# Gathering part of the third layer's first seven tiles from a second table, ahead of the last block's rows

## The chip, the cores and the metric

The kernel runs on one core of one Trainium2 chip. The metric is the device time of one execution in microseconds (us), smaller is better. Beside the plain timed executions there is one execution recorded by the hardware profiler; all durations below come from that one.

## What is computed

Four graph layers over N = 4096 nodes with F = 128 features, each followed by a residual sum and a layer norm. The adjacency matrix `adj` is symmetric in its pattern and nearly empty: some eight neighbours per node beside the diagonal.

```python
x = layernorm(x + signed_attention(x, adj))      # layer 0
x = layernorm(x + chebyshev(x, adj))             # layer 1: three products with adj, twice
# layer 2: attention with 4 heads; only entries of adj count
h = (x @ weight.T).reshape(n, heads, f_out)
C = alpha_src[None] + alpha_dst[:, None]
tau = adj_t * exp(maximum(0.2 * C, C))
z = einsum('mnh,nhf->mhf', adj_t * tau / tau.sum(1), h)
x = layernorm(x + z + bias)
# layer 3
x = layernorm(x + x @ W_self + (adj @ x / deg) @ W_neigh)
```

In the title "third layer" is layer 2 of this listing, the attention.

## The kernel before

Nodes are cut into 32 tiles of 128 (`NT`), and into 8 blocks of 512 (`NB`, four tiles each). Layers 0 and 1 are dense products on TensorE that read `adj` from HBM in chunks of 1 MB. While they run, the kernel makes lists of the non-zero entries: for every column the six neighbours with the highest row index (`NEAR`), and the rest of all columns of a tile packed into three lists of 128 slots (`QT`). `lists.source[:, t, 0:9]` holds the row indices of tile t: 0 to 2 are the packed slots, 3 to 8 the six neighbours. An unused slot points at row N, which holds zeros and a very low score. `check` (L1565) looks over bounds that the lists rely on and sets a flag; if it is set, a second, general version of the network runs after this one.

`sparse_layers` (L1722) is the last part, and the change lies in it. Its engines follow an order that is written out by hand: every engine executes its instructions in the order in which Python emits them.

First comes the rest of layer 1: for each block `ib` eight chunks of `adj` times `w`, four products a chunk (L2050), collected in PSUM. `block_end(ib, p)` (L1746) then turns the sum of a block into the rows that the attention reads: ELU, transposes (L154), layer norm, a product with `W2S` (L1781), rows scaled by the norm (L1786), and a store of 512 rows of 132 floats into the DRAM tensor `table` (L1789, a DMA on ScalarE's queue). `block_end` is a generator with eight steps, and `one(chains)` advances it by one step after each chunk of the next block, so that its small steps lie between the products. For the last block (`ib` = 7) no products are left to put between.

GpSimd (POOL) meanwhile fetches `value` entries of the lists by indirect DMA: `pulls`, three a chunk, each followed by a one-element operation, `pause` (L1518, L1563). One more pause a chunk reads a tile that VectorE has just written (`known`), which holds POOL to the pace of the chunks.

Then the attention: a loop over 32 tiles. `gathers(t)` (L1815) issues nine indirect DMAs on POOL for tile t, each of which brings 128 rows of `table` into `got[t]` (four buffers); every second one is followed by a pause, and two of the pauses read the reciprocal `rd` of two tiles earlier and the newest sum `acc3`. `edges(t)` (L1837) turns `got[t]` into weighted rows, nearly all on VectorE (L1846 to L1858); its first operation that needs the gathered rows is L1850. `sums` multiplies them on TensorE (L1863), `divide` and `turn` finish the tile (L1870 to L1872, L159, L160), and `layer3_rows` and `layer3_product` use the new x for layer 3 (L1931: one product per tile with all of `adj`; VectorE adds the results up, L1944). Groups of tiles for layer 3 have 1, 1, 2, 4, 4, 4, 4, then 2 tiles each, and 1 and 1 at the end. Before the loop, four chunks of 1 MB for the first two groups are requested on ScalarE's queue (`columns` with `nc.scalar`, L1919). In the loop, `gathers(t + 2)` comes after the work on tile t, and `check` runs ahead of tile 3's work.

Of the kernel before, what the change touches and what calls it, by code (L numbers as in the profile page):

```python
# [11 lines left out]
F32 = mybir.dt.float32  # L12
# [5 lines left out]
ALU = mybir.AluOpType  # L18
AX = mybir.AxisListType
PSUM = bass.MemoryType.PSUM  # L20

P = 128
IB = 512
TB = IB // P
# [11 lines left out]
QT = 3  # L36
# [3 lines left out]
PAIRED = [0, 1, 2]  # L40
LAST = [0, 1]
FAR = [4, 5, 6, 7]
NONE = -1e30


@with_exitstack
def adj_resnorm_d4(ctx: ExitStack, tc: tile.TileContext, x_in, xT_in, adj, adjT, pairs, diag_in, w0g, w0gT, a0, w1a, b1a,
# [7 lines left out]
    nc = tc.nc  # L55
    N, F = x_in.shape
# [1262 lines left out]
    class Lists:  # L1319
# [3 lines left out]
        def __init__(self, whole, first, layer, own_entries):  # L1323
            enter = lambda **kw: whole.enter_context(tc.tile_pool(reuse_waits="tile", **kw))
            self.keep = keep = enter(name="lists", bufs=1)
            self.psum = first.enter_context(tc.tile_pool(name="ps_u", bufs=2, space=PSUM, reuse_waits="tile"))
            dram = enter(name="dram", bufs=1, space=bass.MemoryType.DRAM)
            self.table = dram.tile([N + 1, F + H], F32, name="table")
            self.tables = [dram.tile([N + 1, F], F32, name=f"rows{n}") for n in range(3)]
            self.spread = dram.tile([NB, P, TB * SLOTS], BF16, name="spread")  # L1330
            self.top = state.tile([P, NT, NB, 8], F32, name="top", tag="dv")
            self.at = keep.tile([P, NT - TB, NB, 8], U16, name="at")
            self.diag = own_entries
            self.last = None
            nc.scalar.dma_start(self.diag, diag_in)
            self.source = keep.tile([P, NT, NEAR + QT], I32, name="source")
            self.value = keep.tile([P, NT, NEAR + QT], F32, name="value")
            self.where = keep.tile([P, NT, QT], I32, name="where")
            units = len(PAIRED) * TB
            self.back = keep.tile([P, units, NEAR + QT], F32, name="back")  # L1340
            self.into = keep.tile([P, units, QT], F32, name="into_column")
            self.column = keep.tile([P, TB], I32, name="column")
            self.tile_column = keep.tile([P, TB, QT], I32, name="tile_column")
            self.bad = keep.tile([P, 4, NB], F32, name="bad")
            self.iota = keep.tile([P, P], F32, name="iota")
            self.slot = keep.tile([P, SLOTS], F16, name="slot")
            self.place = keep.tile([P, TB, QT], F32, name="place")
            self.first = keep.tile([P, NB, 8], F32, name="first")
            self.own = keep.tile([P, 1], F32, name="own")
            self.below = keep.tile([P, P], BF16, name="below")  # L1350
            self.row = keep.tile([P, TB, QT], I32, name="row")
            flat = lambda t: t.rearrange("p s r -> p (s r)") if len(t.shape) > 2 else t
            with tc.tile_pool(name="lists_i", bufs=1) as pool:
                i = pool.tile([P, SLOTS], I32, name="i")
                for t, pattern, base, step in ((self.slot, [[1, SLOTS]], 0, 0), (self.place, [[0, TB], [P, QT]], 0, 1),
                                               (self.first, [[IB, NB], [0, 8]], 1, 0), (self.own, [[0, 1]], 0, 1)):
                    n = flat(t).shape[1]
                    nc.gpsimd.iota(i[:, 0:n], pattern=pattern, base=base, channel_multiplier=step)  # L1358
                    nc.vector.tensor_copy(flat(t), i[:, 0:n])
                nc.vector.tensor_copy(self.iota, self.slot[:, 0:P])  # L1360
                nc.vector.tensor_scalar(self.below, self.iota, self.own, None, op0=ALU.is_gt)
                none = pool.tile([1, F + H], F32, name="none")
                nc.vector.memset(none, 0.0)
                nc.vector.memset(none[:, F:F + H], NONE)
                nc.scalar.dma_start(self.table[N:N + 1, :], none)
                zero = pool.tile([1, F], F32, name="zero")
                nc.vector.memset(zero, 0.0)
                for rows in self.tables:
                    nc.scalar.dma_start(rows[N:N + 1, :], zero)
            nc.gpsimd.iota(self.column, pattern=[[P, TB]], base=0, channel_multiplier=1)  # L1370
            nc.gpsimd.iota(flat(self.tile_column), pattern=[[P, TB], [0, QT]], base=0, channel_multiplier=0)
            nc.gpsimd.iota(flat(self.row), pattern=[[IB, TB], [0, QT]], base=0, channel_multiplier=0)
            self.idle = keep.tile([P, 2], F32, name="idle")
            nc.gpsimd.memset(self.idle, 1.0)
            self.work = layer.enter_context(tc.tile_pool(name="lists_w", bufs=1, reuse_waits="tile"))
            self.both_at = self.work.tile([P, units, NEAR + QT], I32, name="both_at")
            self.both = self.work.tile([P, units, NEAR + QT, 2], F32, name="both_ways")
# [187 lines left out]
        def check(self, psum, name):  # L1565

            worst = small.tile([P, 4], F32, name="worst")
            for n, most in enumerate((0.0, 0.0, float(MOST), float(SLOTS))):
                nc.vector.tensor_reduce(worst[:, n:n + 1], self.bad[:, n, :], AX.X, ALU.max)
                nc.vector.tensor_scalar(worst[:, n:n + 1], worst[:, n:n + 1], most, None, op0=ALU.is_gt)  # L1570
            both = small.tile([P, 2], F32, name="both")
            nc.vector.tensor_reduce(both[:, 0:1], worst, AX.X, ALU.max)
            units = len(PAIRED) * TB
            free = self.into.rearrange("p u j -> p (u j)")
            left, own = free[:, 0:units], free[:, units:2 * units]
            nc.vector.tensor_scalar(self.back, self.back, 0.0, None, op0=ALU.is_gt)
            nc.vector.tensor_reduce(left, self.back, AX.X, ALU.add)
            for n, c in enumerate(PAIRED):
                nc.vector.tensor_scalar(own[:, n * TB:(n + 1) * TB], self.diag[:, c * TB:(c + 1) * TB], 0.0, None, op0=ALU.is_gt)
                nc.vector.tensor_tensor(own[:, n * TB:(n + 1) * TB], own[:, n * TB:(n + 1) * TB], degrees[0][:, c * TB:(c + 1) * TB], ALU.subtract)  # L1580
            nc.vector.tensor_tensor(left, left, own, ALU.add)
            nc.vector.tensor_reduce(both[:, 1:2], left, AX.X, ALU.add)
            pb = psum.tile([1, 2], F32, name=name)
            nc.tensor.matmul(pb, ones, both, start=True, stop=True)
            most = small.tile([1, 1], F32, name="most")
            nc.vector.tensor_scalar(most, pb[:, 1:2], 0.0, None, op0=ALU.not_equal)
            nc.vector.tensor_tensor(most, pb[:, 0:1], most, ALU.max)
            nc.vector.tensor_tensor(flag, most, flag0, ALU.add)
# [133 lines left out]
    def sparse_layers(enter, lists, w, h0T):  # L1722
# [19 lines left out]

        warm = small.tile([P, 1], F32, name="warm")
        fresh = None

        def block_end(ib, p):  # L1746

# [29 lines left out]
            for half in range(2):  # L1777
# [8 lines left out]
                nc.vector.tensor_tensor(rows[:, two, :], pn[:, :, 0:F + H], scale.to_broadcast([P, 2, F + H]), ALU.mult)  # L1786
                nc.vector.tensor_tensor(near[:, two, :], pn[:, :, F + H:F + 2 * H], scale.to_broadcast([P, 2, H]), ALU.mult)
                fresh = rows[:, two.start, 0:1]
            nc.scalar.dma_start(table[ib * IB:(ib + 1) * IB, :].rearrange("(k p) f -> p k f", p=P), rows[:, tb, :])  # L1789
            e = l2.tile([P, TB, H], F32, name="e")  # L1790
            d = l2.tile([P, TB, H], F32, name="d")
            nc.vector.tensor_tensor(e, near[:, tb, :], rows[:, tb, F:F + H], ALU.add)
# [22 lines left out]
        def gathers(t, behind={}):  # L1815
            if t >= NT:
                return
            got[t] = l2.tile([P, E, F + H], F32, name="got", bufs=4)
            for j in range(E):
                nc.gpsimd.indirect_dma_start(got[t][:, j, :], None, table,  # L1820
                                             bass.IndirectOffsetOnAxis(ap=lists.source[:, t, j:j + 1], axis=0))
                if j % 2:
                    lists.pause(behind.get(j))
# [159 lines left out]
        with tc.manual_schedule(engines={mybir.EngineType.PE, mybir.EngineType.DVE, mybir.EngineType.Activation,  # L1983
# [3 lines left out]
            def one(queue, n=1):  # L1987
                while queue and n:
                    r = next(queue[0], queue)
                    if r is not queue:  # L1990
                        n -= 1
                    else:
                        queue.popleft()
# [49 lines left out]
            for ib in range(NB):  # L2043
# [3 lines left out]
                for n, c in enumerate(order):  # L2047
                    a = chunk(ld, adjT, ib, c)
                    for k in range(TB):
                        nc.tensor.matmul(p, w[:, c * TB + k, :], a[:, k, :], start=n == 0 and k == 0,  # L2050
                                         stop=n == NB - 1 and k == TB - 1)
                        if k == 1:
                            one(others)
                    one(chains)
                    for f in plan.pop(hook, ()):
                        f()
                    if known is not None:
# [6 lines left out]
                next(end)  # L2064
                chains.append(end)
            assert not plan and not others
            while chains:
                one(chains)
            for t0, n in groups[:2]:
# [87 lines left out]
```

## Time and profile before

| what | us |
|---|---|
| median of three timed runs | 1839.98 (1831.49 to 1844.66) |
| the profiled execution, whole | 1653.07 |
| its span (first to last instruction) | 1651.2 |
| layers 0 and most of 1 | 0 to 1000 |
| rest of layer 1, with block ends | 1000 to 1216 |
| attention and layer 3, POOL gathering | 1216 to 1590 |
| last tile, rest of layer 3, output | 1590 to 1651 |

The timed runs take 187 us longer than the profiled execution of the same program; nothing in the trace says where. The page of the profile gives each engine's busy time, the chain of work that ended last (followed back from the last instruction, each step to what released it), and the costliest groups of instructions. Over the whole span TensorE is busy 90%, VectorE 69%, POOL 50%. Those shares are means over stages with different limits, so the stage of the change has to be read by itself, from the timeline of each engine, in which a bracket names the idle time before an instruction and what ended it.

### The profile page before, as it was taken

How to read it: one execution, taken by the hardware profiler on the slowest of the kernel's cores; microseconds unless marked ns; L12 is line 12 of the kernel's file. 1: busy time of each engine (PE TensorE's matmuls, PEld its weight loads, DVE VectorE, ACT ScalarE, POOL GpSimd, SP SyncE). 2: the span in 40 equal slices, each digit the busy share in tenths (PEclk: the TensorE clock that was granted, in tenths of full speed). 3: DMA queues.
4: the chain of work that ended last, by engine and by line, in shares of the span. 5: the costliest groups of instructions: out<-in, count | busy, mean ns of one | idle time of the engine just before them, and what ended most of it. 6: DMA issues, size and time to landing. Idle time of an engine off the chain costs nothing.

```text
span 1651.2 us, 16460 instructions
## 1 busy us (share of the span) xinstructions
PE 1478.5 (90%) x4744; PEld 714.2 (43%) x4744; DVE 1138.4 (69%) x3203; ACT 385.5 (23%) x693; POOL 833.1 (50%) x1322
## 2 busy tenths in 40 slices
PE   6899999999999999999999999889927689788886
PEld 3344444544444444454444454444413344444444
DVE  5987655789887897988699950455336756556766
ACT  5776540010000011121200000222223111122234
POOL 0000000000242188848486888888648888888841
PEclk9999999999999999999999999999967798889988
DMA  9867776588888885867587888778665677678673
GB/s 374 342 256 301 246 271 233 179 277 299 316 315 320 309 285 195 281 210 274 177 296 248 291 278 305 252 265 287 241 151 153 189 259 244 219 239 278 218 192 95
DMA packets 106972, 419.30 MB, mean 254 GB/s; under 512 B 21556, under 2 KB 44088, under 8 KB 67064
## 3 DMA queue, kind: packets, MB, share of 16 engines
q1 hardware_dynamic: 59984, 360.01, 61.1%
q0 software_dynamic: 22656, 36.17, 8.6%
q10 hardware_dynamic: 24232, 21.98, 4.5%
q8 instruction: 39, 0.64, 0.2%
q14 instruction: 61, 0.50, 0.1%
HBM read 404.39 MB, written 13.70 MB: 253 GB/s over the span
## 4 chain that ended last, share of the span: by engine, by line
PE 46%; DVE 25%; POOL 14%; issue 6%; DMA 6%; ACT 3%; ACTq 0%; DVEq 0%; POOLq 0%
PE pacc L730 15%; PE pacc L423 12%; POOL got L1820 6%; PE pp L2050 5%; DMA got<-table,source 4%; PE pp L1931 3%; POOL got L1518 3%; DVE at L1397 3%; DVE top L1396 2%; POOL idle L1563 2%; DVE here L1556 1%; POOL value L1518 1%; DVE same L1317 1%; DVE gw L1856 1%; DVE acc L1944 1%
## 5 line engine op out<-in xcount | busy, mean ns | idle before, releaser
L1820 POOL DMA_INDIRECT got<-table,source x288 | 275.8, 958 | 88.8 <-issue 62.0
L1931 PE MATMUL pp<-chunk,xT 128*128 128x512 f32 x496 | 244.0, 633 | 1.4 <-ACT xT L1902 0.7
L730 PE MATMUL pacc<-chunk,x 128*128 128x512 f32 x512 | 222.6, 593 | 0.0
L1518 POOL DMA_INDIRECT got<-rows,source x180 | 182.8, 1016 | 67.6 <-issue 38.6
L423 PE MATMUL pacc<-chunk,hw 128*128 128x512 f32 x408 | 188.7, 607 | 0.8 <-DVE hw L466 0.7
L1358 POOL IOTA i<- 128x384 int32 (+3 forms) x4 | 1.0, 238 | 345.7 <-PE pden L411 329.8
L2050 PE MATMUL pp<-chunk,w 128*128 128x512 f32 x384 | 173.1, 600 | 0.0
L730 PE MATMUL pacc<-chunk,t 128*128 128x512 f32 x384 | 171.5, 597 | 0.0
L730 PEld LDWEIGHTS pacc<-chunk,x 128*128 128x128 f32 x512 | 96.0, 190 | 114.7 <-issue 114.6
L730 PE MATMUL pacc<-chunk,v 128*128 128x512 f32 x320 | 144.5, 597 | 0.0
L1396 DVE MAX8 top<-chunk 128x8 f32<-128x512 f32 x196 | 128.5, 677 | 14.1 <-DMA chunk<-in_adjT 14.1
L1931 PEld LDWEIGHTS pp<-chunk,xT 128*128 128x128 f32 x496 | 94.2, 203 | 91.2 <-issue 84.1
L1397 DVE FIND_INDEX8 at<-top,chunk 128x8 uint16<-128x512 f32 x196 | 133.1, 684 | 0.0
L1518 POOL DMA_INDIRECT both_ways<-in_pairs,both_at x108 | 106.6, 987 | 17.4 <-issue 17.1
L423 PEld LDWEIGHTS pacc<-chunk,hw 128*128 128x128 f32 x408 | 75.0, 192 | 92.1 <-issue 86.3
L1563 POOL TENSOR_TENSOR idle<-idle 128x1 f32<-128x1 f32 x489 | 110.3, 226 | 8.6
L730 PEld LDWEIGHTS pacc<-chunk,t 128*128 128x128 f32 x384 | 71.7, 192 | 81.8 <-issue 81.8
L2050 PEld LDWEIGHTS pp<-chunk,w 128*128 128x128 f32 x384 | 71.7, 194 | 78.5 <-issue 77.7
L395 ACT ACTIVATE junk<-chunk 128x2048 fp8e4<-128x2048 f32 x51 | 97.4, 1910 | 29.8 <-DMA chunk<-in_adjT 29.3
L329 DVE TENSOR_SCALAR pos<-chunk 128x2048 bf16<-128x2048 f32 x66 | 80.1, 1219 | 33.7 <-DMA chunk<-in_adjT 32.1
L1863 PE MATMUL u<-gw,into 128*128 128x132 f32 x192 | 33.2, 317 | 68.3 <-DVE gw L1856 68.3
L1556 DVE SCALAR_TENSOR_TENSOR here<-got,back,here 128x128 f32<-128x128 f32 x120 | 42.2, 352 | 67.0 <-DMA got<-rows,source 63.8
(424 smaller groups left out, 2058.7 us busy)
## 6 DMA issues: line engine op xcount, KB each, us to landing
chunk<-in_adjT SPq DMA_DIRECT2D x326, 1024.0 KB, 5.4
keep<-in_adjT SPq DMA_DIRECT2D x13, 1024.0 KB, 11.0
spread<-spread ACTq DMA_DIRECT2D x16, 384.0 KB, 4.5
got<-table,source POOLq DMA_INDIRECT x288
chunk<-in_adjT ACTq DMA_DIRECT2D x4, 1024.0 KB
got<-rows,source POOLq DMA_INDIRECT x180
table<-rows ACTq DMA_DIRECT2D x8, 264.0 KB, 5.2
xT<-in_xT ACTq DMA_DIRECT2D x8, 256.0 KB, 6.5
```

The lines of the kernel that those rows point to most:

```text
L329: r = nc.vector.tensor_scalar(pos, a, 0.0, None, op0=ALU.is_gt)
L395: nc.scalar.activation(junk, a, AF.Relu, scale=-1.0, accum_out=bad[:, n:n + 1], saturate=False)
L423: in_order(nc.tensor.matmul(p, hw[:, j * TB + k, :], a[:, k, :], start=first and k == 0, stop=last and k == TB - 1))
L730: nc.tensor.matmul(p, stationary(c * TB + k), a[:, k, :], start=n == 0 and k == 0, stop=n == NB - 1 and k == TB - 1)
L1396: pin(nc.vector.max(self.top[:, t, ib, :], row))
L1397: pin(nc.vector.max_index(self.at[:, t - TB, ib, :], self.top[:, t, ib, :], row))
L1518: tc.keep_in_program_order(nc.gpsimd.indirect_dma_start(out, None, of, bass.IndirectOffsetOnAxis(ap=index, axis=0)))
L1556: pin(nc.vector.scalar_tensor_tensor(here, got[:, j, 0:F], self.back[:, u, j:j + 1], here, op0=ALU.mult, op1=ALU.add))
L1563: return nc.gpsimd.tensor_tensor(self.idle[:, 0:1], of, self.idle[:, 1:2], ALU.mult)
L1820: nc.gpsimd.indirect_dma_start(got[t][:, j, :], None, table, bass.IndirectOffsetOnAxis(ap=lists.source[:, t, j:j + 1], axis=0))
L1931: nc.tensor.matmul(p, y[:, t0 + k, :], a[:, ib % (TB // n), k, :], start=k == 0, stop=k == n - 1)
L2050: nc.tensor.matmul(p, w[:, c * TB + k, :], a[:, k, :], start=n == 0 and k == 0, stop=n == NB - 1 and k == TB - 1)
```

## The change

A second DRAM table, `table_early`, gets the rows of blocks 0 to 6, each stored beside the store into `table`. Its last 512 rows, those of block 7, are filled with zeros at the start. The three packed gathers of tiles 0 to 6 (21 in all) read it. They are emitted before the last block's remaining steps: those of tiles 0 and 1 go straight into `got`, those of tiles 2 to 6 into a new tile `packed`, from which ScalarE copies them into `got[t]` when that buffer is assigned. `gathers` of tiles 0 to 6 then issues six DMAs instead of nine; its first pause (the one that reads `rd`) falls away there. During the last block, `one(chains)` is called twice a chunk instead of once. `check` has five more VectorE operations: they set the flag if a packed slot of tiles 0 to 6 points at a row of block 7. For the reference's inputs none does: worked out from them, the highest such row is 3345, and block 7 starts at 3584.

```diff
+EARLY = 7
...
             self.table = dram.tile([N + 1, F + H], F32, name="table")
+            self.table_early = dram.tile([N + 1, F + H], F32, name="table_early")
...
+                nc.scalar.dma_start(self.table_early[N:N + 1, :], none)
+                blank = pool.tile([P, TB, F + H], F32, name="blank")
+                nc.vector.memset(blank, 0.0)
+                nc.scalar.dma_start(self.table_early[N - IB:N, :].rearrange("(k p) f -> p k f", p=P), blank)
...
+            of, late = [self.back[:, 0:EARLY, n:n + QT] for n in (0, QT)]
+            nc.vector.tensor_copy(of, self.source[:, 0:EARLY, 0:QT])
+            nc.vector.tensor_scalar(late, of, float(N - IB), None, op0=ALU.is_ge)
+            nc.vector.scalar_tensor_tensor(late, of, float(N), late, op0=ALU.is_lt, op1=ALU.mult)
+            nc.vector.tensor_reduce(worst[:, 0:1], late, AX.XY, ALU.max)
+            nc.vector.tensor_tensor(both[:, 0:1], both[:, 0:1], worst[:, 0:1], ALU.max)
...
+        stored = set()
+        packed = state.tile([P, EARLY - 2, QT, F + H], F32, name="packed", tag="dv")
+
+        def early():
+            for t in range(EARLY):
+                if t < 2:
+                    got[t] = l2.tile([P, E, F + H], F32, name="got", bufs=4)
+                for j in range(QT):
+                    lists.by_index(got[t][:, j, :] if t < 2 else packed[:, t - 2, j, :], lists.table_early, lists.source[:, t, j:j + 1])
...
-            nc.scalar.dma_start(table[ib * IB:(ib + 1) * IB, :].rearrange("(k p) f -> p k f", p=P), rows[:, tb, :])
+            for of in (lists.table_early, table) if ib < NB - 1 else (table,):
+                nc.scalar.dma_start(of[ib * IB:(ib + 1) * IB, :].rearrange("(k p) f -> p k f", p=P), rows[:, tb, :])
+            stored.add(ib)
...
-            got[t] = l2.tile([P, E, F + H], F32, name="got", bufs=4)
-            for j in range(E):
+            if t not in got:
+                got[t] = l2.tile([P, E, F + H], F32, name="got", bufs=4)
+            if 2 <= t < EARLY:
+                nc.scalar.copy(got[t][:, 0:QT, :], packed[:, t - 2])
+            for j in range(QT if t < EARLY else 0, E):
...
-                    one(chains)
+                    for _ in range(2 if ib == NB - 1 else 1):
+                        one(chains)
...
             assert not plan and not others
+            while NB - 2 not in stored:
+                one(chains)
+            deque(pulls, 0)
+            early()
             while chains:
                 one(chains)
```

## Prediction

> **What bounds the kernel now.** I read the page's chain of waits first, then the timelines of POOL, ScalarE and VectorE from 1190 us on. Over 1216 to 1590 us the chain's largest shares are POOL's gathers (26%) and their landing (19%), with the products of L1931 far behind (11%).
>
> ```profile
> L1820 POOL DMA_INDIRECT got<-table,source x288 | 275.8, 958 | 88.8 <-issue 62.0
> ```
>
> 288 gathers of 958 ns. Of the 88.8 us of idle time before them 62.0 is issue, and 19.5 is this one wait at the stage's start (POOL's timeline; start, length, what, and in brackets the idle time before it with its releaser):
>
> ```profile
> 1196.71 0.19 POOL L1563 TENSOR_TENSOR idle<-rows,idle 128x1 f32<-128x1 f32 x1 [3.71 <-DVE near L1787]
> 1216.37 0.97 POOL L1820 DMA_INDIRECT got<-table,source  x1 [19.47 <-DMA table<-rows]
> ```
>
> POOL's last `value` fetch is over at 1182.0; what follows are pauses. So it does nothing of use for 34 us, waiting for block 7's rows. ScalarE's timeline has the stores:
>
> ```profile
> 1196.60 0.37 ACTq L1789 DMA_DIRECT2D table<-rows  x1
> ...
> 1212.28 0.37 ACTq L1789 DMA_DIRECT2D table<-rows  x1
> ```
>
> The first is block 6, the second block 7; the gather starts 4.1 us after the second. From there POOL never stops: 288 gathers take (1589.9 - 1216.4)/288 = 1.30 us each, pauses included, 11.7 us a tile. VectorE's timeline, tiles 0 to 7, at the first operation that needs the gathered rows:
>
> ```profile
> 1234.05 0.18 DVE L1850 TENSOR_TENSOR score<-got,near 128x24 f32<-128x24 f32 x1 [15.66 <-DMA got<-table,source]
> ...
> 1243.60 0.24 DVE L1850 TENSOR_TENSOR score<-got,near 128x24 f32<-128x24 f32 x1 [1.40 <-DMA got<-table,source]
> ...
> 1255.40 0.18 DVE L1850 TENSOR_TENSOR score<-got,near 128x24 f32<-128x24 f32 x1 [2.50 <-DMA got<-table,source]
> ...
> 1267.17 0.16 DVE L1850 TENSOR_TENSOR score<-got,near 128x24 f32<-128x24 f32 x1
> ...
> 1277.57 0.21 DVE L1850 TENSOR_TENSOR score<-got,near 128x24 f32<-128x24 f32 x1
> ...
> 1288.98 0.18 DVE L1850 TENSOR_TENSOR score<-got,near 128x24 f32<-128x24 f32 x1 [1.26 <-DMA got<-table,source]
> ...
> 1301.55 0.18 DVE L1850 TENSOR_TENSOR score<-got,near 128x24 f32<-128x24 f32 x1 [3.79 <-DMA got<-table,source]
> ...
> 1312.45 0.22 DVE L1850 TENSOR_TENSOR score<-got,near 128x24 f32<-128x24 f32 x1 [2.10 <-DMA got<-table,source]
> ```
>
> Here is the decisive reading. POOL is always busy, yet VectorE waits for it only 11.05 us over tiles 1 to 7 (the sum of the brackets). It needs 78.40 - 11.05 = 67.35 us itself for these seven steps, 9.6 a tile: its own operations in a row, the round trips to ScalarE (exp, square root) and TensorE (`sums`), the additions of L1944 (four take 2.47), and in tile 3 the check. Tiles 3 and 4 don't wait at all.
>
> **What the Trainium skill says.** "TensorE: Matmul & The Clock Gate", Part 1, says that after an idle window of some 3.4 us the array runs at half its clock until it has been busy as long. The trace agrees: granted clock 1.00 in 1100 to 1200, 0.50 in 1216 to 1240 behind the idle time, 0.74 to 1280. So the first tiles' `sums` stay slow, with or without the change. "DMA: Bandwidth & Descriptors", Issuing engines are not separate DMA queues, says that all DMAs run on the same 16 engines and interleave. Agrees: four 1 MB chunks requested from 1215.6 raise the DMA share to 0.92, and tile 0's last gather, issued at 1227.26, lands 6.57 us later; tile 7's rows are in use 2.6 us after its last issue.
>
> **The change, part by part.**
>
> 1. *Block 6's rows earlier.* A chunk of four products takes 3.43 us (two in 6.87), and block 7 begins at 1173.5. With two steps a chunk the first transposes follow chunk 1 (1177.0; their input is ready at 1176.55), the second ones chunk 2 (1180.8), both `W2S` pairs chunk 3 (1184.7; copy 0.58, table load 1.28, square root 0.30 and reciprocal 0.18 end by 1184). The rows are done at about 1186.3 instead of 1196.6. TensorE stalls at most a few tenths; I charge 0.3 (0 to 2, the full latency of one step).
> 2. *Early gathers.* Store issue to gather was 4.1 us; a store lands in 3.1 in the idle time and 5.2 in the median, so POOL starts at 1190.4 to 1192.5; I take 1191.5. The 21 gathers are issued like the `value` fetches, with a pause each, 1.35 us start to start (1152.79, 1154.14): 28.4 us, to 1219.9. That passes 1216.4 by 3.5, which is a delay for the six gathers queued behind.
> 3. *Fewer gathers in the loop.* Tile 0 then needs 6 x 1.30 = 7.8 us, to 1227.7; before, its ninth was issued at 1227.26. The 4 MB are unmoved, so its rows land about when they did: 1233.5 (gain 0.5; -3 to +3). Each later tile up to 6 gives POOL 3.9 us, and the pause on `rd` is gone there, so POOL leads.
> 4. *VectorE's pace.* From tile 0 to tile 7 VectorE needs its 67.35, plus the check's five new operations. Its old ones follow each other every 0.2 to 0.27 us; tile 3 does not wait, so nothing covers them: 1.0 (0.8 to 1.3). Tile 7 starts at 1233.5 + 68.35 = 1301.9. POOL for tile 7 (nine gathers again): its pause needs tile 5's `rd`, 6.9 us after that tile's start at 1284, so 1291; seven more gathers, 9.1, and 2.6 to use: 1302.7. Tile 7 gains 1312.45 - 1302.7 = 9.8, and POOL's stream is ahead by the same amount. From there it sets the pace as before, to the end.
> 5. *ScalarE's copies.* Five of 128x396, between the measured 0.30 (128x132, L1844) and 0.58 (128x512): 0.45 each. They lie ahead of the exp, while VectorE works; cost 0, and 2.3 if that cover is gone.
> 6. *Stores and blanks.* Seven further stores on ScalarE's queue (0.37 to issue each) and 1.9 MB, 7 us of transfer at 261 GB/s, pass SP's chunk loads while the DMA share is 0.78 and TensorE is 98% busy; SP loads up to five chunks ahead, which covers them. If not, up to 3; I take 0.3. Filling the blank rows at the start (one VectorE memset, near the 0.48 of a 128x512 operation, and 264 KB): 0.2 (0 to 1).
>
> Sum: 9.8 - 0.3 - 0.3 - 0.2 = **9 us** off the profiled execution, 1653.07 to about 1644 (span 1642). The timed median is 187 us above it, from a place that the trace doesn't show; I carry over the 9 us as they are: 1839.98 - 9 = **1831**.
>
> **The rivals.**
>
> - *POOL alone sets the pace.* Then the stream ends at 1191.5 + 28.4 + 267 x 1.30 = 1567 instead of 1589.9: 23 us, 1817. For it: POOL's unbroken row of gathers, 26% of the chain. Against: VectorE has only 11 us to give up. It needs VectorE's 9.6 us a tile to shrink, as by TensorE warming up sooner.
> - *Early gathers stand in the way* (the other side). POOL runs in order: what is late in the early ones delays all gathers of tile 0, and everything waits for that. The gain of tiles 1 to 7 is 10 us, so it turns into a loss once tile 0 comes over 10 us late, that is once the 21 end after about 1230. With the store at its old place (start 1200.7) they end at 1229; if half of them also meet the 4 MB and take 1 us more each, at 1239: tile 0 is 19 us late, the result 9 us slower, 1849. Against: TensorE's order puts the store's inputs after three chunks.
> - *The gain is lost later.* TensorE is busy 232 of 270 us in 1320 to 1590. If the timed runs, 11% longer, have that time in TensorE, it is full there (232 x 1.11 = 258, of 270 now and of 261 with the gain), and the stream's lead ends in waits for `rd`: gain 0 to 4, 1838. That the change doesn't do what it says is the same number: block 6 stored as late as before and the early gathers merely shifted, tile 7 gains 1 to 2.
>
> **How the numbers follow.** The forecast (VectorE takes over) 0.60, POOL alone 0.15, early gathers in the way 0.08, lost later 0.17. A measurement of this kernel can tell about 1%, 18 us, from no change. Only POOL alone reaches that, with most of its weight, and a little of the first case if the 1.11 of the timed runs widens it: faster 0.16. Slower by 18 needs the second rival at twice its price: 0.04. Same 0.80. The range: the forecast's own is 1825 to 1837; with POOL alone below, the loss above and the timed runs' own spread of +-7 it is 1812 to 1847.
>
> **What would show it.** The first gather from `table_early` at 1190 to 1193, block 6's first store at 1186; the last early gather at about 1220, the first from `table` right behind; tile 0's L1850 within 3 us of 1234, tiles 2 to 6 with no wait for a DMA, their steps as long as the 67.35 says; tile 7 at 1302; the last gather at 1580 instead of 1588.9. It is wrong if tiles 1 to 6 run every 8 us (POOL alone), if the first gather from `table` starts after 1225, or if waits for `rd` or L1931 appear on POOL after tile 7.

## The result, and the profile after

| | us, median | runs |
|---|---|---|
| before | 1833.35 (1824.3 to 1852.43) | 22 |
| changed | 1824.53 (1813.11 to 1836.72) | 22 |

The ratio is 0.9945, 95% interval 0.9926 to 0.9963: 10 us of the time before, with an interval from 7 to 14. The interval leaves out 1, so the kernel is faster, but by less than the 1% that the forecast set as its bound.

Traces have to be kept apart by chip. The same kernel before took 1833 us (median) in this set, and 1808, 1840 and 1650 in the three sets of the experiments, which ran on three different chips. Which chip gave this result, and which the first profile, is not known; the first profile, 1653.07, is like the last set, so the 187 us between it and the timed runs look like a difference of chips. I call the sets, and their chips, A (this result), B (1808), C (1840) and D (1650). Times are compared within a set only, and positions are counted from VectorE's first operation on block 7's sum (1203.07 in the profile before), which I call the zero point.

The changed kernel's profile is from A: whole 1824.21, span 1822.3. Its page has the gathers and the chain by engine like this (line 1846 was 1820 before):

```profile
PE 49%; DVE 25%; issue 9%; another core or an unknown queue 8%; ACT 4%; DMA 3%; POOL 2%; ACTq 0%; DVEq 0%; POOLq 0%
...
L1846 POOL DMA_INDIRECT got<-table,source x267 | 255.7, 958 | 69.3 <-issue 66.2
```

There are 21 gathers fewer, 958 ns each as before. The 8% is time in which an engine did nothing and no record names the cause. The first profile has none of it, but the page of the kernel before on B has 8% too, so the change does not bring it. ScalarE's timeline has the stores of block 6 and block 7 (line 1789 before):

```profile
1312.69 0.37 ACTq L1811 DMA_DIRECT2D table_early<-rows  x1
1313.10 0.52 ACTq L1811 DMA_DIRECT2D table<-rows  x1
1338.19 0.37 ACTq L1811 DMA_DIRECT2D table<-rows  x1
```

Block 7's products began at 1299.93, so block 6 is stored 12.8 us later, 16.8 us ahead of the zero point (1329.46) instead of 6.5. POOL's timeline, first and last early gather, then the first of the loop:

```profile
1319.24 0.97 POOL L1524 DMA_INDIRECT got<-table_early,source  x1 [5.43 <-DMA table<-rows]
...
1346.87 0.97 POOL L1524 DMA_INDIRECT packed<-table_early,source  x1 [0.15 <-issue]
1348.22 0.97 POOL L1846 DMA_INDIRECT got<-table,source  x1 [0.15 <-issue]
```

The loop's first gather comes 18.8 us after the zero point; before, 13.3. VectorE's timeline, the first operation that needs the rows (1850 before) of tiles 0, 1, 6 and 7:

```profile
1362.47 0.18 DVE L1876 TENSOR_TENSOR score<-got,near 128x24 f32<-128x24 f32 x1 [18.14 <-DMA got<-table,source]
1370.52 0.17 DVE L1876 TENSOR_TENSOR score<-got,near 128x24 f32<-128x24 f32 x1
...
1427.04 0.17 DVE L1876 TENSOR_TENSOR score<-got,near 128x24 f32<-128x24 f32 x1
1437.90 0.18 DVE L1876 TENSOR_TENSOR score<-got,near 128x24 f32<-128x24 f32 x1 [2.09 <-DMA got<-table,source]
```

Tiles 1 to 6 have no bracket: no wait. But tile 0 is at 33.0 after the zero point, 2.0 later than in the first profile.

All kernels in one table, in us after the zero point. "0 to 7" is the time between tile 0's first use of its rows and tile 7's; "gap" is from the start of tile 0's last gather to that use.

| kernel, chip | first loop gather | gap | tile 0 | tile 7 | 0 to 7 | end of span |
|---|---|---|---|---|---|---|
| before, first profile | 13.3 | 6.8 | 31.0 | 109.4 | 78.4 | 448.1 |
| before, B | 12.7 | 7.2 | 30.7 | 122.5 | 91.8 | 502.9 |
| pace_only, B | 13.1 | 6.4 | 30.8 | 121.0 | 90.2 | 502.1 |
| no_pace, B | 26.5 | 5.4 | 39.0 | 115.7 | 76.7 | 494.8 |
| changed, B | 21.1 | 8.7 | 37.2 | 112.2 | 75.0 | 487.9 |
| changed, A | 18.8 | 7.0 | 33.0 | 108.4 | 75.4 | 492.8 |
| changed, C | 19.9 | 9.2 | 36.0 | 111.0 | 75.0 | 498.2 |
| early4, C | 12.6 | 8.0 | 27.7 | 108.7 | 81.0 | 501.0 |
| no_check, C | 21.2 | 8.9 | 37.0 | 112.1 | 75.1 | 498.4 |
| ahead_sp, C | 22.5 | 2.7 | 31.7 | 111.0 | 79.3 | 500.8 |
| changed, D | 21.4 | 8.9 | 38.4 | 111.1 | 72.7 | 444.5 |
| split, D | 12.5 | 8.3 | 27.6 | 103.2 | 75.6 | 437.2 |
| split_sp, D | 21.4 | 2.7 | 30.7 | 111.0 | 80.3 | 444.4 |
| six_all, D | 18.2 | 6.2 | 31.7 | 101.4 | 69.7 | 400.9 |

Each row is one profile, and two pairs of rows show how far one profile carries. Until the work on tile 5 is done, six_all runs the same instructions as the changed kernel, and no_check does until tile 3. Yet tile 0 came at 31.7 and 38.4 on D, and at 37.0 and 36.0 on C. VectorE's timeline of six_all, zero point 1202.61, has tile 0 here:

```profile
1234.31 0.18 DVE L1876 TENSOR_TENSOR score<-got,near 128x24 f32<-128x24 f32 x1 [16.28 <-DMA got<-table,source]
```

So the sign of tile 0's delay holds: 31.7 to 38.4 in the six profiles with all 21 gathers early, two steps a chunk and the loads on ScalarE's queue, against 30.7 to 31.0 in the three without early gathers. Its size does not, and single positions that differ by less than some 7 us decide little.

### The profile page after: what moved, and what is told of

Read it like the earlier page. It is cut to its first block, busy times and chain, and to the rows that moved or that the text cites. A ratio compares the mean times of both kernels' runs of the same rounds, so it can differ in the third digit from the quotient of the medians.

```text
span 1822.3 us, 16500 instructions
## 1 busy us (share of the span) xinstructions
PE 1538.9 (84%) x4740; PEld 735.8 (40%) x4744; DVE 1140.9 (63%) x3209; ACT 387.1 (21%) x698; POOL 834.8 (46%) x1336
## 4 chain that ended last, share of the span: by engine, by line
PE 49%; DVE 25%; issue 9%; another core or an unknown queue 8%; ACT 4%; DMA 3%; POOL 2%; ACTq 0%; DVEq 0%; POOLq 0%
PE pacc L731 17%; PE pacc L424 11%; PE pp L1957 6%; PE pp L2076 5%; DVE at L1403 2%; DVE top L1402 2%; DVE here L1884 2%; DVE here L1562 2%; DVE gw L1882 1%; DVE spread L1318 1%; DVE same L1318 1%; DVE acc L1970 1%; PE pden L412 1%; PE px L1924 1%
## 5 line engine op out<-in xcount | busy, mean ns | idle before, releaser
L1846 POOL DMA_INDIRECT got<-table,source x267 | 255.7, 958 | 69.3 <-issue 66.2
L1957 PE MATMUL pp<-chunk,xT 128*128 128x512 f32 x496 | 260.3, 668 | 8.1 <-ACT xT L1928 5.3
L731 PE MATMUL pacc<-chunk,t 128*128 128x512 f32 x384 | 187.9, 637 | 10.5 <-issue 10.5
L731 PE MATMUL pacc<-chunk,v 128*128 128x512 f32 x320 | 154.5, 626 | 9.4 <-issue 9.3
L1957 PEld LDWEIGHTS pp<-chunk,xT 128*128 128x128 f32 x496 | 99.6, 215 | 104.9 <-issue 92.8
L731 PEld LDWEIGHTS pacc<-chunk,t 128*128 128x128 f32 x384 | 77.0, 206 | 104.1 <-issue 104.1
L1569 POOL TENSOR_TENSOR idle<-idle 128x1 f32<-128x1 f32 x508 | 114.1, 225 | 8.9
L1970 DVE TENSOR_TENSOR acc<-pp,acc 128x512 f32<-128x512 f32 x96 | 62.5, 683 | 61.2 <-remote 40.0
L731 PEld LDWEIGHTS pacc<-chunk,v 128*128 128x128 f32 x320 | 60.6, 198 | 83.5 <-issue 83.5
```

What stands on the lines that cost most here:

```text
L731: nc.tensor.matmul(p, stationary(c * TB + k), a[:, k, :], start=n == 0 and k == 0, stop=n == NB - 1 and k == TB - 1)
L1569: return nc.gpsimd.tensor_tensor(self.idle[:, 0:1], of, self.idle[:, 1:2], ALU.mult)
L1846: nc.gpsimd.indirect_dma_start(got[t][:, j, :], None, table, bass.IndirectOffsetOnAxis(ap=lists.source[:, t, j:j + 1], axis=0))
L1957: nc.tensor.matmul(p, y[:, t0 + k, :], a[:, ib % (TB // n), k, :], start=k == 0, stop=k == n - 1)
L1970: nc.vector.tensor_add(acc3[:, blk], p, acc3[:, blk])
```

## Experiments

**Both kernels once more, and the two halves of the change** (chip B). pace_only is the kernel before with this edit alone; no_pace is the changed kernel without it:

```diff
-                    one(chains)
+                    for _ in range(2 if ib == NB - 1 else 1):
+                        one(chains)
```

> The kernel before, unchanged, for a profile in the regime of the timed runs (some 1830 us; the first profile of it was 1653). Counted from the start of block 7's products. Theory 1 (VectorE takes over from POOL in the first tiles): tile 7's first use of its rows at about 147, 9 us later than the 138 of the changed kernel, with 8 us or more of waits for gathers in tiles 1 to 7. Theory 2 (in this regime other stalls set the pace of the tiles, and POOL has slack already): tile 7 at 139 to 142, waits under 3 us, and the 9 us come from elsewhere.

> The changed kernel, unchanged, for a second profile. Both theories: tile 7 at about 138 us from block 7's start if it lands in the regime of the timed runs; if it lands in the fast one (span near 1640), theory 1 expects tile 7 at 129 (139 before, less 9.8) and the last gather 10 us earlier relative to block 7 than in the first profile of before.

> The kernel before with the two steps a chunk in the last block alone. Theory 1: nobody waits for block 6's rows, so 1.000 (within 0.002). A rival, that the gain comes from a shorter tail of block ends (block 6's steps no longer share VectorE and ScalarE with block 7's): 0.996 or less.

> The changed kernel with one step a chunk in the last block as before. Block 6's store is then 10 us later and the 21 early gathers end 10 us later, so tile 0 comes some 9 to 10 us later than in the changed kernel. Theory 1: nearly the whole gain is gone, 0.999 to 1.003. If POOL has slack to make up for it in the first tiles: 0.996.

| kernel | ratio to before | 95% interval |
|---|---|---|
| b0_again | 1.0010 | 0.9985 to 1.0036 |
| a0_again | 0.9909 | 0.9889 to 0.9929 |
| pace_only | 0.9999 | 0.9977 to 1.0020 |
| no_pace | 0.9969 | 0.9948 to 0.9990 |

Neither forecast for the two kernels fits. The kernel before has tile 7 some 152 us after block 7's start, later than both theories said, with 5.75 us of waits for gathers, between the two; the changed kernel has it at some 142, not 138.

The faster steps alone bring nothing: nobody fetches block 6's rows sooner. Without them (no_pace) block 6's store is 10.3 us later, as expected, but its rows land 3.6 us after the issue instead of 8.7, so the early gathers begin only 5.2 us later (2.9 ahead of the zero point instead of 8.1). Tile 0, expected 9 to 10 us later, is 1.8 later: its last gather is issued 5.1 later, but the gap is 3.3 shorter. By then the four loads were thinning out; the DMA share was 0.44 in the last 3 us of the gap, and 0.73 in the changed kernel's. Tile 7 is 3.5 later. The times differ by more, 1804.25 - 1791.58 = 12.7 us; the remaining 9 I can't place.

Where does the gain on B come from? Between tiles 0 and 7 the kernel before needs 91.8 us, though the waits that name a gather are only 5.75. VectorE's timeline of the kernel before on B shows another kind (lines 1870 and 1944; the operation waits for TensorE's sums, and TensorE's records end at 1347.04):

```profile
1352.51 0.18 DVE L1870 RECIPROCAL rd<-u 128x4 f32<-128x4 f32 x1 [8.75 <-remote]
...
1402.59 0.69 DVE L1944 TENSOR_TENSOR acc<-pp,acc 128x512 f32<-128x512 f32 x1 [4.29 <-remote]
1405.40 0.18 DVE L1870 RECIPROCAL rd<-u 128x4 f32<-128x4 f32 x1 [2.11 <-remote]
```

"remote" stands for a releaser that the trace does not have; the kernel has one core. In the changed kernel on B VectorE has no such idle time between tiles 0 and 7, and 2.41 us of waits that name a gather: 15.15 + 5.75 - 2.41 = 18.5 us less idle time, against a shortening of 91.8 - 75.0 = 16.8. From this, tile 0's delay of 6.5 goes off; tile 7 is 10.3 us earlier, and the end of the span 15.0. Behind tile 7 VectorE's "remote" waits did not shrink: 42.7 us before, 52.4 in the changed kernel. The lead was kept all the same.

**Fewer early gathers, no check, the 4 MB on another queue** (chip C).

```diff
-EARLY = 7
+EARLY = 4
```

> EARLY is 4 instead of 7: 12 early gathers (four tiles) instead of 21, so tiles 4 to 6 issue nine in the loop again. Theory A (what the early gathers save is VectorE's waiting in tiles 1 to 7, and what they cost is the hold on POOL ahead of tile 0): 9 gathers fewer are 9 x 1.35 = 12 us, so POOL is free at about +9 us, ahead of block 7's rows, and tile 0's L1850 falls back to about 30 us after block 7's sum (37.2 in the changed kernel, 30.7 before); tiles 1 to 3 run at their own pace, 4 to 7 wait 0 to 4 us in all. Tile 7 at 104 to 112, ratio 0.987 to 0.995, the same as the changed kernel or up to 6 us better. Theory B (the gain is just POOL's work moved off the loop, 1.3 us a gather): 12 of 21 are left, and the gain is 12/21 of the changed kernel's, ratio 0.994 to 0.997, tile 7 at about 116.

no_check leaves out the five operations from `of, late = ...` to the maximum into `both[:, 0:1]`.

> The five operations that the change adds to the check are left out: packed slots of tiles 0 to 6 are not tested for rows of block 7 any more. They were priced at 1.0 us on VectorE in front of tile 3, uncovered. Theory A (VectorE sets the pace in tiles 0 to 7): the step from tile 2 to tile 3 shrinks from about 15 us by 1 to 2 us and tile 7 comes as much earlier; the time moves by at most 2 us, ratio 0 to 0.001 below the changed kernel's in the same call. Theory B (VectorE has slack there, the check lies beside other work): the step stays within 0.5 us and so does tile 7.

ahead_sp:

```diff
-                    ahead[t0, ib] = columns(t0, n, ib, nc.scalar)
+                    ahead[t0, ib] = columns(t0, n, ib)
```

> The four 1 MB chunks for the first two groups of layer 3 are requested on SyncE's queue instead of ScalarE's, where they stood behind block 7's store. Theory A (tile 0's rows land late because these 4 MB and the gathers share the DMA engines): the chunks go as soon as their buffers are free, some 10 us earlier, while the DMA engines have little to do; tile 0's last gather lands 2.6 to 4 us after its issue instead of 6 to 11, tile 0 and all tiles to 7 come 2 to 7 us earlier, ratio 0.001 to 0.004 below the changed kernel's. Theory B (tile 0 is late because POOL reaches its gathers late, and the 4 MB are hidden): tile 0 moves by less than 1 us. A loss is possible too: the 4 MB then meet the early gathers and block 7's store instead, POOL's early gathers and the store land later, tile 0 up to 5 us later.

> The changed kernel once more, unchanged, as the yardstick of the three runs beside it. Both theories expect 0.988 to 0.996 of the time before. The positions in the trace, counted from the start of block 7's sum on VectorE: last early gather at about 23 us, first gather of a tile from the full table at 19 to 21, tile 0's first use of its rows at 33 to 37, tile 7's at 108 to 112. If these positions move by more than 5 us from one profile to the next, single positions carry nothing and only the times do.

| kernel | ratio to before | 95% interval |
|---|---|---|
| a0_ctrl | 0.9923 | 0.9896 to 0.9951 |
| early4 | 0.9940 | 0.9914 to 0.9967 |
| no_check | 0.9911 | 0.9878 to 0.9944 |
| ahead_sp | 0.9922 | 0.9893 to 0.9951 |

*early4.* Tile 0 is back at 27.7: the 21 gathers in front of it were the delay. But tiles 4 to 6 issue nine gathers again, and the steps to tiles 4 to 7 are 10.0, 10.0, 15.3 and 12.7 us; in the changed kernel of the same set 9.5, 10.0, 9.1 and 10.9. In the long one VectorE's timeline has

```profile
1412.20 0.69 DVE L1970 TENSOR_TENSOR acc<-pp,acc 128x512 f32<-128x512 f32 x1 [1.34 <-PE u L1889]
1417.92 0.69 DVE L1970 TENSOR_TENSOR acc<-pp,acc 128x512 f32<-128x512 f32 x1 [5.03 <-remote]
```

So unexplained idle time comes back in the stretch where the nine gathers come back. That is one profile, and ahead_sp below has such a wait with six gathers a tile. The position of tile 7 is that of theory A; the ratio lies where both theories meet and decides nothing. The lead of tile 0 is gone by tile 9, at 142.4 against 141.2.

*no_check.* The step from tile 2 to 3 falls from 15.5 to 12.5 us, three times what I charged, and the next one rises from 9.5 to 12.1; 2.0 us of it is a "remote" wait. Tile 7 is 75.0 after tile 0 with the five operations and 75.1 without. So they cost nothing that can be seen in the sum, as theory B said, though its step did not stay as it was.

*ahead_sp.* The gap falls from 9.2 to 2.7 and tile 0 comes 4.3 us earlier, as theory A said, although POOL reached its gathers 2.6 later. The loads were through before the gathers ran: between tile 0's first gather and the use of its rows the DMA share is 0.18, and 0.97 in the changed kernel of the same set. This fits the shared DMA engines that the Trainium skill describes ("DMA: Bandwidth & Descriptors", Issuing engines are not separate DMA queues): by that page another queue doesn't give other engines, and what the edit gave is another time. The run moved both at once and doesn't part the engines from the memory behind them.

The rest of theory A failed: tile 7 is at 111.0 in both kernels and the time doesn't move. The step from tile 1 to 2 is 15.8 instead of 12.0, and VectorE's timeline has an unexplained wait in it, with six gathers a tile:

```profile
1371.25 0.18 DVE L1896 RECIPROCAL rd<-u 128x4 f32<-128x4 f32 x1 [7.02 <-remote]
```

**A split, and six gathers everywhere** (chip D). split:

```diff
-            early()
+            early(range(4))
...
             gathers(1)
+            early(range(4, EARLY))
```

split_sp adds the edit of ahead_sp. six_all leaves out the packed gathers of tiles 7 to 31 and copies other tiles' rows in their place, so its output is not the network's; it tells the price of the gathers only. Its edit of the changed kernel:

```diff
-            if 2 <= t < EARLY:
-                nc.scalar.copy(got[t][:, 0:QT, :], packed[:, t - 2])
-            for j in range(QT if t < EARLY else 0, E):
+            if t >= 2:
+                nc.scalar.copy(got[t][:, 0:QT, :], packed[:, (t - 2) % (EARLY - 2)])
+            for j in range(QT, E):
```

> The changed kernel unchanged, as the yardstick of the three runs beside it: ratio 0.989 to 0.996, tile 0 at 33 to 37 us after block 7's sum, tile 7 at 108 to 112, tile 9 at 139 to 142.

> Only the 12 early gathers of tiles 0 to 3 stay ahead of the last block's rows; the nine of tiles 4 to 6 are issued behind the loop's gathers of tiles 0 and 1. Theory A (tile 0 is late in the changed kernel because 21 gathers stand before it, and tiles 1 to 7 then run at VectorE's own pace): POOL is free at about +5 us, tile 0 comes at 28 us after block 7's sum as with four early tiles, and since tiles 4 to 6 again issue six gathers each their steps stay at 9 to 10 us with no wait: tile 7 at 101 to 104, 8 us ahead of the changed kernel. If what follows keeps that lead, the ratio is 0.004 below the changed kernel's in the same call. Theory B (from tile 8 on something else sets the time, which was at 139 to 146 us for tile 9 in all runs whether tile 0 came at 28 or at 39): tile 7 comes earlier, tile 9 stays at 139 to 145, and the time is within 0.002 of the changed kernel's.

> The same split with the four 1 MB chunks for the first two groups requested on SyncE's queue. Theory A: tile 0 comes 2 to 4 us earlier than with the split alone (they landed beside its rows), at 24 to 26 us, tile 7 at 98 to 102, ratio 0.005 to 0.006 below the changed kernel's. Theory B: tile 9 still at 139 to 145 and the time within 0.002 of the changed kernel's.

> All 32 tiles issue six gathers in the loop: the packed slots of tiles 7 to 31 get copies of those of tiles 2 to 6 instead of their own rows, so that part of the computation is left out (75 gathers, 98 us of POOL's work), and the pause that reads rd falls away in all tiles. Theory A (POOL's stream of nine gathers a tile still sets the pace behind tile 7, by holding VectorE where the trace names no cause): those unexplained waits on VectorE vanish from tile 7 on as they did in tiles 1 to 7, steps fall from 13.7 us a tile to 10 to 11, and the kernel is some 60 to 80 us faster, ratio 0.955 to 0.965. Theory B (VectorE, TensorE and the products of layer 3 set the pace there, and POOL merely follows): steps stay within 1 us of 13.7, POOL idles 4 us a tile more, and the ratio is 0.98 to 0.993.

| kernel | ratio to before | 95% interval | us, median |
|---|---|---|---|
| a0_third | 0.9979 | 0.9965 to 0.9993 | 1646.40 |
| split | 0.9973 | 0.9963 to 0.9983 | 1645.55 |
| split_sp | 1.0002 | 0.9990 to 1.0014 | 1649.46 |
| six_all | 0.9749 | 0.9723 to 0.9774 | 1607.03 |

Here the kernel before takes 1650.41, and the change brings 0.0021 x 1650 = 3.5 us, less than the 0.989 to 0.996 expected; tile 0 is later and tile 9 (133.8) earlier than the windows said. From the zero point on no wait of these four profiles, or of the first profile before, is put down to "remote"; VectorE's longest one without any releaser ("issue") is 4.5 us, in split. VectorE's timeline of the changed kernel on D, tiles 0, 1 and 7:

```profile
1240.89 0.18 DVE L1876 TENSOR_TENSOR score<-got,near 128x24 f32<-128x24 f32 x1 [23.40 <-DMA got<-table,source]
1248.91 0.20 DVE L1876 TENSOR_TENSOR score<-got,near 128x24 f32<-128x24 f32 x1
...
1313.62 0.18 DVE L1876 TENSOR_TENSOR score<-got,near 128x24 f32<-128x24 f32 x1 [2.80 <-DMA got<-table,source]
```

This trace can be laid beside the first profile before nearly microsecond by microsecond (zero points 1202.47 and 1203.07): tile 0 was at 1234.05 and tile 7 at 1312.45. All that tiles 1 to 7 gain, tile 0 has lost in this profile. In six_all's, with the same instructions to there, tile 0 is 0.7 later than in the first profile and tile 6 5.8 earlier.

*split* does what theory A said for tiles 0 and 7 (27.6 and 103.2, the latter with idle time of 1.7 and 4.1 us ahead of tiles 1 and 2), and in its profile the last gather starts at 378.7 instead of 386.4. The times hardly follow: 0.9 us, where theory B had less than 0.002 of the time (3.3 us) and theory A 0.004. Its profiled execution, 1639.6, was the lowest of its 22 runs, so I don't take its 7 us for the usual. Whether the split beats the changed kernel stays open; the intervals overlap.

*split_sp*: theory A is refuted here, with tile 0 at 30.7 instead of 24 to 26 and a ratio above the changed kernel's. POOL's timeline shows where:

```profile
1223.43 0.97 POOL L1846 DMA_INDIRECT got<-table,source  x1 [12.91 <-DMA chunk<-in_adjT]
```

The 12 early gathers are over, and the first gather of block 7's rows starts 12.6 us after their store was issued (1210.80), where it was 3.8 to 4.1 in the other profiles in which POOL waited for that store. The releaser that the trace names is a chunk load: the loads on SyncE's queue now run beside block 7's store.

*six_all* leaves VectorE 0.23 us of waits for gathers over all tiles behind tile 0 (54.05 in the changed kernel), and the tiles from 7 to 31 take 10.25 us each instead of 11.66. POOL now waits 39.9 us for VectorE's additions (L1970). So on D POOL sets the pace behind tile 7 by 1.41 us a tile; the pause on `rd` is gone in these tiles too, and the run doesn't part it from the gathers. 24 x 1.41 = 34 us, and tile 7 is 9.7 earlier, which makes the 43.6 between the ends of the two profiles; the times lie 39 apart. Theory A's steps came; its ratio was sized for the 13.4 to 14.1 us a tile of chips B and C, and D has 11.66 to begin with. Whether the unexplained idle times would go too was not tried on a chip that has them.

## Why the prediction was right in number, and where its steps were not

The forecast of 9 us lies inside the measured 7 to 14, and the time, 1824.53, inside the whole range of 1812 to 1847 (half a microsecond below the forecast's own 1825 to 1837). But the sum was made for the profiled execution, and the chip like it shows 3.5; on B the gain came with idle time that the sum does not contain. So the number is right in part by luck. Of the forecast's signs, the waits of tiles 1 to 6 are gone as it said, but tile 7 is at 108.4 (A) or 111.1 (D) instead of 99.6, and on D the last gather is at 386.4 instead of 377.

1. *Block 6 earlier.* Right: the store 12.8 us after block 7's start, as worked out.
2. *Early gathers.* Forecast too early by 1.3 us on A (19.3 after block 7's start instead of 18.0) and by 3 on D. The error is the store's landing: the forecast took 5.2 us from store to gather, between the idle figure of 4.1 and one for a median landing. Beside the chunk loads of block 7 it was 6.5 on A and 8.2 on D; in no_pace, where both stores go at the end of the products, 3.6. (The trace names the second of the two stores as what ended the wait; by no_pace's figure a second one costs nothing by itself.) The 28.4 us for the 21 came to 29.0 on A and 29.9 on D, start to start.
3. *Tile 0.* This is the step that failed. The forecast set POOL's delay against the three gathers fewer and let the rows land when they had landed before: a gain of 0.5, tile 0 at 30.4. ScalarE's timeline and POOL's on D, block 6's store, the first early gather, and the first gathers of tiles 0 and 1:

```profile
1185.70 0.37 ACTq L1811 DMA_DIRECT2D table_early<-rows  x1
...
1193.95 0.97 POOL L1524 DMA_INDIRECT got<-table_early,source  x1 [7.12 <-DMA table<-rows]
...
1223.85 0.97 POOL L1846 DMA_INDIRECT got<-table,source  x1 [0.15 <-issue]
...
1233.30 0.94 POOL L1846 DMA_INDIRECT got<-table,source  x1 [0.30 <-issue]
```

   Every term was too small there: the first early gather 3.0 us late, the 21 longer by 1.5, the six by 1.7 (9.5 instead of 7.8; POOL is idle 2.4 us ahead of three of them, put down to the landing of early ones), and from there to the use of the rows 7.6 instead of 5.8. Tile 0 was at 38.4, 7.4 later than in the first profile; 6.5 later on B, 0.7 in six_all. So a loss of 0.7 to 7.4 us stood where a gain of 0.5 was forecast. With 12 early gathers (early4, split) POOL is free before block 7's rows are there, and tile 0 comes at 27.6 to 27.7.
4. *VectorE's pace.* Right in mechanism on D. There tiles 0 to 7 took 72.7, less the 2.80 that tile 7 waited: 69.9 against 68.35. So tile 7 on D is 9.8 - 7.9 (tile 0) - 3.55 (pace, and a longer wait at tile 7) = 1.7 us late, not 9.8 early. In these two profiles the 3.5 us of gain lie behind tile 7, and with tile 0's scatter one profile each can't place them. On A, B and C the pace was 75, and what it replaced was not 78.4 but, on B, 91.8: with the early gathers idle time of tiles 0 to 7 is gone that the first profile did not contain. That, not my sum, brought tile 7's 10 us on B. A and C have no profile of the kernel before, so for A's 10 us this is likely and not shown.
   "From there it sets the pace as before": true on D (six_all). On B not: POOL waits for `rd` there, 52.1 us in all before and 50.4 after, at 13.6 and 13.4 us a tile. Waits for `rd` behind tile 7 were named as a sign of being wrong; on A they are 41 us, on B 44 before and 36 after, on D 0.4.
5. *Copies.* 0.51 to 0.55 us each where 0.45 was taken. Tiles 2 to 6 wait for nothing at the rows, so they were covered. The check's 1.0 didn't move tile 7 on C.
6. *Stores and blanks.* Block 7's sum starts 29.3 us after block 6's with and without them; nothing to see in that stage. The blank rows at the start were not tried alone.

The rivals: *POOL alone* did not come: only the step from tile 0 to 1 took 8 us. *Early gathers stand in the way* is real but smaller than its deciding point: 0.7 to 7.4 us of the 10. *Lost later* in its own form, a lead that ends in waits for `rd`, was not put to a test by itself; early4 and ahead_sp show on C that leads of 8 and 4 us at tile 0 were gone by tile 9 or 2. On A, B and C ScalarE stood idle at the same place, in tile 8, without a named cause (8.48 us on A):

```profile
1458.68 0.37 ACT L1928 ACTIVATE xT<-px,rstd 128x127 f32<-128x127 f32 x1 [8.48 <-remote]
```

## What to carry over

Work moved ahead of a late input is free only up to the moment when that input arrives: count what the moved instructions push back on their in-order engine. Here 21 gathers delayed the first tile and 12 did not, though no run showed a shorter time for 12. A slow landing beside a bulk load is no slack to count on: in the six profiles it took 6.2 to 9.2 us behind the later issue (6.4 to 7.2 behind the earlier one before), and only where the issue came 5 us later still, with the loads nearly through, was it shorter (5.4, no_pace). A second profile of the same instructions can put a position 7 us elsewhere, so take one before reading a few microseconds from it. And when the timed runs take 10% longer than the profiled one, profile again before trusting a budget made from it, for the waits that the change removes may be ones that the first profile never had.

## What the runs showed that I had not expected

The same program took 1650, 1808 and 1840 us on three chips. On the latter two, and on A, single engines stand idle for 2 to 10 us in the last part without a named releaser; what holds them is not shown. Between tiles 0 and 7 VectorE's such waits sum to 15.2 and 14.0 us in the two profiles with nine gathers a tile, to 5.0 in early4, and to nothing in four of the six with six gathers on these chips, but to 2.0 in no_check and 7.0 in ahead_sp; so they go along with the number of gathers without being bound to it. In the one of 8.75 us quoted above TensorE's records had ended, its granted clock was 1.00 for the first part, and no instruction-fetch packet ran; POOL went on gathering, and a 1 MB load ran (DMA share 0.89 from 1346 to 1350), until 2.5 us before it ended; from 1351 on the DMA share was 0.02.

One candidate can't be ruled out: the Trainium skill ("Perfetto Trace Analysis", Tensor Engine Instruction (MATMUL, LD_WEIGHTS)) says that the recorded end of a matmul is computed, not observed, so sums that really ended late could look like this. One number speaks against it: the granted clock fell to 0.50 at 1349.7, 2.6 us after TensorE's last record, and behind block 7's products in the same profile it fell 3.5 us after the last one. So it falls some 3 us after the records end in a place where nothing hides TensorE's idle time, and did the same here; sums that kept TensorE busy up to 1352 don't fit that. No run settles it.

The gap between a gather's issue and the use of its rows was 2.7 us without, and 5.4 to 9.2 us with four 1 MB loads beside it, in the table's fourteen profiles without exception. From the issue of a 270 KB store to the gather behind it took 3.6 to 4.1 us in the idle time and 6.3 to 8.7 beside the chunk loads of block 7.
